# Attention outputs of a chunked linear-attention head as two 64-query halves in the array shape of k^T v

## The chip, the cores and the metric

The kernel runs on one core of a Trainium2 chip. Its time is that of one execution on the device in microseconds (us); three runs were made, and their median is the time before. The engines are TensorE (PE; its weight loads are listed as PEld), VectorE (DVE), ScalarE (ACT), GpSimd (POOL) and SyncE (SP, which issues the DMAs).

## The reference, cut to what matters

The program is a transformer block with adaptive layer norm on an input of 2 batches x 4096 tokens x 256 channels. Its attention part is two layers of a recurrent model (time mix and channel mix each), its second part a gated FFN with blockwise 4-bit rounding of inputs and weights. The change touches the recurrence of the time mix, for each of 4 heads of 64 channels:

```python
def step(state, inp):
    rt, kt, vt, wt = inp
    kv = kt[..., :, None] * vt[..., None, :]
    out = jnp.einsum('bhk,bhkv->bhv', rt, state + u[None, :, :, None] * kv)
    return (state * wt[..., None] + kv, out)
```

So each token's output is r times (the state of all earlier tokens plus the bonus u times its own k v^T), and the state decays by w per channel and takes k v^T in. Each head's output is then normalised over its 64 values.

## The kernel before, in words

Work is cut into tiles of 256 tokens (`TT`), 16 per batch and layer, and each tile into two chunks (`C`) of 128 tokens. With two layers and two batches there are 64 passes through the recurrence; one such pass of one tile, with all four heads, is called a head section here. The four heads stand in two pairs (`J`), a pair in the 128 partitions.

**Order of the work.** The kernel writes no instruction directly. Generators (one stream per batch and layer, and some for the FFN and the loading of weights) record operations through `Recorder` and `Plan.record` (L237); `Plan.run` (L342) chooses, again and again, the operation that can start first by its own table of costs (`weight`, L422, the latencies in `Plan.LAT`, and `TURN` and `BACK`, what a change of array shape costs) and issues it through `give_out` (L283, the call at L294, which is the line of almost all instructions in the profile). Calls to TensorE that one stream records without another engine's call or a `yield` between them become one operation and are issued in one burst. Each engine takes its instructions in the order issued. What the planner's table says of costs decides the order of all engines, not of the changed part alone.

**The head section** is `wkv` (L845). The streams take turns in it by `head_lock` while it is recorded. The decayed r and k are built level by level on VectorE; products of 32 or 64 keys with 16 to 64 queries land in the PSUM tile `pa`; masked copies put them, through `diag`, into `attn` (L675), a tile [128 keys, pair member p, chunk c, pair j, 128 queries] in SBUF. Four transposes (L936) bring k^T-to-be into a bank, and ScalarE copies it to `kt` (L939).

Then come (L950 to L975):
- `kv`: for each chunk, pair and head p, kt (128 tokens x 64) against v (128 x 64). The result of head p lies in partitions 64p to 64p+63, so the product uses 128 rows and 64 columns of the array, and the two heads of a pair use its two column halves.
- `po`, one PSUM bank of two chunks x 256: for each chunk and pair, r times the state S (a 128x128 product with 128 moving columns, which opens the accumulation), then per head attn (128 keys x 128 queries, the full array) times v (64 moving columns) on top.
- per chunk, after its outputs: the update of S on VectorE, S * decay + kv; chunk 1's r times S needs that of chunk 0. Then the square of the chunk's outputs on ScalarE and its sum per head on VectorE.

After both chunks: the power -1/2 on POOL, the scaling on VectorE, and back in `time_mix` transposes, the gate and the product with Wo.

All of it is fp32. A product in fp32 is seen in the trace as two records of weight load and two of matmul.

Of the kernel before, what the change touches and what calls it, by code (L numbers as in the profile page):

```python
# [11 lines left out]
BF16 = mybir.dt.bfloat16  # L12
I32 = mybir.dt.int32
AF = mybir.ActivationFunctionType
ALU = mybir.AluOpType
AX = mybir.AxisListType
PSUM = bass.MemoryType.PSUM

P = 128
D = 256  # L20
J = D // P
TT = 256
C = TT // P
HS = 64
H = D // HS
# [92 lines left out]
class Plan:  # L118
# [118 lines left out]
    def record(self, eng, fn, a, k):  # L237
        st = self.cur
        outs = [k["out"]] if "out" in k else [a[0]]
        ins = list(a[0 if "out" in k else 1:]) + [v for n, v in k.items() if n != "out"]  # L240
        ins = [v for v in ins if isinstance(v, (bass.AP, Later))]
        cost, port = weight(eng, fn, outs[0], ins)
        op = st.last if eng == "tensor" else None
        if op is None or op.next is None:
            self.count += 1
            op = Op(eng, self.count)
            op.rank = op.age + self.random.uniform(0.0, JITTER)
            op.late = st.late
            st.queue.append(op)
        st.last = op if eng == "tensor" else None  # L250
        op.calls.append((getattr(getattr(self.nc, eng), fn), a, k))
        f = form(eng, fn, outs[0], ins, a)
        if f is not None:
            if op.forms and op.forms[-1] != f:
                op.cost += self.TURN[eng]
            op.forms.append(f)
        op.cost += cost
        op.port = op.port or port
        for v in ins:
            if not is_dram(v):  # L260
                self.need(op, v, False)
        for v in outs:
            if not is_dram(v):
                self.need(op, v, True)
# [157 lines left out]
def weight(eng, fn, out, ins):  # L422


    def psum(v):
        return isinstance(v, Later) or v.name.startswith(("pa", "kv"))

    n = max(v.free_size() for v in [out] + ins)
    if eng == "tensor":
        n, rows, cols = out.free_size(), ins[0].shape[0], out.shape[0]  # L430
        if fn == "transpose":
            return 110.0, False
        if rows == P and cols == P:
            return max(4 * n / 2.4 + 6, 195.0 if n == 64 else 265.0 if n == P else 0.0), False
        if n <= 64:
            return {(64, 32): 18.0, (64, 64): 65.0, (P, 64): 65.0}.get((rows, cols), 2 * n), False
        return 0.57 * (4 * n / 2.4 + 6), False
    if eng == "sync":
        return 100.0, False
    wide = [v for v in ins if v.free_size() > 1]  # L440
    if eng == "scalar":
        return 180.0 + n / 1.2 + (85.0 if len(wide) < len(ins) else 0.0), False
    if eng == "gpsimd":
        if out.free_size() <= 8:
            return 360.0 + 170.0 * n, False
        return 90.0 + 2.1 * n, True
    two = sum(not psum(v) for v in wide) >= 2
    if fn in ("tensor_scalar", "tensor_copy"):
        two = not any(psum(v) for v in wide)
        if out.dtype == I32:  # L450
            return 145.0 + n / 1.92, two
    if fn in ("bn_stats", "bn_aggr", "tensor_reduce", "reciprocal"):
        two = False
    if fn == "reciprocal":
        return 150.0 + 6.2 * n, False
    return (205.0 if fn == "scalar_tensor_tensor" and n <= 256 else 150.0) + n / 0.96, two
# [3 lines left out]
def rwkv_adaln_fp4_kernel(ctx: ExitStack, tc: tile.TileContext, a: dict, out: bass.AP):  # L460
# [13 lines left out]
    nc = tc.nc  # L474
# [5 lines left out]
    const = ctx.enter_context(tc.tile_pool(name="const", bufs=1))  # L480
# [5 lines left out]
    make_identity(nc, ident)  # L486
    nhalf = const.tile([P, C * H], F32, name="nhalf")
    nc.gpsimd.memset(nhalf, -0.5)

# [37 lines left out]
    pl = Plan(nc, banks)  # L529
# [8 lines left out]
    def take_slot():  # L538
        return pl.take(stock)
# [4 lines left out]
    def give(*ts):  # L544
        stock.extend(ts)

    def give2(t):
        stock2.append(t)

    def v3(t, k=2):  # L550
        return t[:, : J * TT].rearrange("p (k n) -> p k n", k=k)

    def v4(t):
        return t[:, : J * TT].rearrange("p (c j t) -> p c j t", c=C, j=J)
# [59 lines left out]
    def halves(ps, k=2):  # L614
        return ps[:, :512].rearrange("p (k n) -> p k n", k=k)
# [38 lines left out]
    rows = {}  # L654
# [20 lines left out]
    attn = keep.tile([P, 2, C, J, P], F32, name="attn")  # L675
# [8 lines left out]
    def mm(o, lhsT, rhs, start, stop):  # L684
        pl.tensor.matmul(o, lhsT, rhs, start=start, stop=stop)
# [10 lines left out]
    head_lock = []  # L696
# [108 lines left out]
    def parts(rk):  # L805

        return (
            rk[:, m * J * TT : (m + 1) * J * TT].rearrange("p (c j t) -> p c j t", c=C, j=J) for m in range(2)
        )
# [35 lines left out]
    def wkv(i, b, rk_s, dec_s, v_s):  # L845

        S = state[i][b]
        rk = rk_s[:, : 2 * J * TT]
        dec, v = v4(dec_s), v3(v_s)
        yield from take(head_lock, (i, b))  # L850
        late = pl.cur.late
# [4 lines left out]
        r, k = parts(rk)  # L856
# [7 lines left out]
        tots_s = take_slot()  # L864
# [22 lines left out]
        for l in range(7):  # L887
            h = 1 << l
# [5 lines left out]
            n = C * J * P // (2 * h)  # L894
# [30 lines left out]
        r, k = parts(rk)  # L925
        tot = tot.rearrange("p (c j) -> p c j", c=C)
        for q in range(4):
            qs = slice(32 * q, 32 * (q + 1))
# [8 lines left out]
        kt_s = take_slot()  # L937
# [4 lines left out]
        o_s, sq_s = take_slot(), take_slot()  # L942
        o_sb, sq = v3(o_s), v3(sq_s)
        bk, po = pl.bank()
        po = halves(po)
        n = C * H
        few = pl.take(tiny)
        rs = few[:, :n]

        for c in range(C):  # L950
            for j in range(J):
                for p in range(2):
                    hd = slice((2 * j + p) * HS, (2 * j + p + 1) * HS)
                    mm(kv[p * HS : (p + 1) * HS, c, j, p * HS : (p + 1) * HS], kt[:, c, hd], v[:, c, hd], True, True)
        yield
        for c in range(C):
            for j in range(J):
                mm(po[:, c, j * P : (j + 1) * P], r[:, c, j, :], S[:, j, :], True, False)
                for p in range(2):
                    hd = slice((2 * j + p) * HS, (2 * j + p + 1) * HS)  # L960
                    mm(po[:, c, hd], attn[:, p, c, j, :], v[:, c, hd], False, p == 1)
            for j in range(J):
                pl.vector.scalar_tensor_tensor(
                    S[:, j, :], S[:, j, :], tot[:, c, j : j + 1], kv[:, c, j, :], ALU.mult, ALU.add
                )
            pl.scalar.activation(sq[:, c, :], po[:, c, :], AF.Square)
            pl.vector.tensor_reduce(
                rs[:, c * H : (c + 1) * H], sq[:, c, :].rearrange("p (h v) -> p h v", v=HS), AX.X, ALU.add
            )
            if c == C - 1:  # L970
                head_lock.clear()
                pl.cur.late = late
                give(kt_s, v_s, sq_s, tots_s)
                give2(rk_s)
            yield  # L975

        pl.vector.tensor_scalar(rs, rs, 1.0 / HS, EPS, ALU.mult, ALU.add)
        pl.gpsimd.tensor_tensor(rs, rs, nhalf[:, :n], ALU.pow)
# [9 lines left out]
    def time_mix(i, b, h):  # L988
# [116 lines left out]
        yield  # L1105

        o_s = yield from wkv(i, b, rk_s, dec_s, v_s)
        bk, pt = to_channels(v3(o_s))
        oT_s = o_s
# [363 lines left out]
```

## Time and profile before

| | |
|---|---|
| runs | 3097.47, 3093.93, 3090.12 us; median 3093.93 |
| span of the profiled execution (its own whole time is not marked among the runs) | 3081.1 us |
| mean granted TensorE clock | 0.981 |
| DMA over the span | 42.56 MB, mean 14 GB/s |
| update of S on VectorE | x256, 340 ns |
| sum of squares per chunk on VectorE (128x4 from 128x256) | x128, 414 ns |
| copy of a 128x512 bank to SBUF on ScalarE | x224, 588 ns |

How to read it: the span runs from the first to the last instruction. A busy share counts an engine as busy while any of its instructions is in flight; matmuls overlap, so their mean duration is a latency, and what a product costs TensorE in a dense row is the distance from its start to the next one's start. In a line of groups, "128*64 128x64 f32" means 128 rows and 64 columns of the array, then partitions and columns of the moving operand. The slices cut the span into 40 equal parts, a digit being tenths of busy time (or of the granted clock).

### The profile page before, as it was taken

The numbers are of one execution on the slowest core, as the hardware profiler recorded it, in microseconds if no ns is written. First come the engines' busy times: TensorE is split into PE (matmuls) and PEld (weight loads), VectorE is DVE, ScalarE is ACT, GpSimd is POOL, SyncE is SP. The second block draws the span as 40 slices with busy tenths as digits, with TensorE's granted clock in tenths as the row PEclk, the third lists the DMA queues.
The fourth block names the chain that finished last, engine by engine and source line by source line (L and its number), as shares of the span: only waits on it lengthen the run. The fifth ranks groups of instructions, "written<-read, shape, count | busy, mean of one in ns | idle before, by whom it ended". The sixth has DMA issues, their size and how long they took to land. (4 is left out here: it accounts for less than half of the span.)

```text
span 3081.1 us, 89987 instructions
## 1 busy us (share of the span) xinstructions
PE 2920.0 (95%) x38460; PEld 2388.7 (78%) x38460; DVE 2345.6 (76%) x6146; ACT 1667.6 (54%) x3478; POOL 1015.7 (33%) x1208
## 2 busy tenths in 40 slices
PE   6899999999999999999999999999999989999997
PEld 4678788777788887888778787787878778787775
DVE  6687876877787877878587777777778776777777
ACT  3465655564565656555564645646456454645452
POOL 2343333333333342333334233242323323232320
PEclk8899999999999999999999999999999999999999
DMA  4000000000000000000000000000000000000000
GB/s 141 12 19 9 15 7 16 3 16 7 13 12 4 20 3 13 11 8 15 5 18 4 10 13 4 19 5 19 4 8 15 3 20 3 6 11 9 9 14 11
DMA packets 35728, 42.56 MB, mean 14 GB/s; under 512 B 2816, under 2 KB 33536, under 8 KB 35328
## 3 DMA queue, kind: packets, MB, share of 16 engines
q1 hardware_dynamic: 35328, 36.81, 3.7%
q8 instruction: 302, 4.95, 0.6%
q14 instruction: 98, 0.80, 0.1%
HBM read 28.41 MB, written 8.39 MB: 12 GB/s over the span
## 5 line engine op out<-in xcount | busy, mean ns | idle before, releaser
L294 POOL TENSOR_TENSOR slot<-slot,slot 128x256 f32<-128x256 f32 (+1 forms) x768 | 578.1, 780 | 819.1 <-DVE slot L294 615.2
L294 ACT ACTIVATE slot<-bank 128x512 f32<-128x512 f32 (+2 forms) x644 | 334.3, 521 | 594.5 <-PE bank L294 563.4
L294 POOL TENSOR_TENSOR tiny<-tiny,nhalf 128x2 f32<-128x2 f32 (+1 forms) x288 | 296.9, 1034 | 874.6 <-DVE tiny L294 852.3
L294 PE MATMUL bank<-slot,cWk 128*128 128x256 f32 x1536 | 364.3, 385 | 4.5 <-DVE slot L294 4.5
L294 PE MATMUL bank<-slot,small 32*128 32x256 f32 (+3 forms) x2816 | 354.9, 359 | 10.3 <-DVE slot L294 6.9
L294 PE MATMUL bank<-cWv,slot 128*128 128x256 f32 x1536 | 342.4, 379 | 0.0
L294 PEld LDWEIGHTS bank<-slot,cWk 128*128 128x128 f32 x1536 | 288.1, 192 | 50.4 <-DVE slot L294 6.5
L294 ACT ACTIVATE slot<-bank,small 128x256 f32<-128x256 f32 (+1 forms) x640 | 250.9, 453 | 138.8 <-PE bank L294 128.7
L294 PEld LDWEIGHTS bank<-cWv,slot 128*128 128x128 f32 x1536 | 290.5, 190 | 39.7 <-issue 0.3
L294 PEld LDWEIGHTS bank<-slot,small 32*128 32x128 f32 (+3 forms) x2816 | 248.5, 178 | 86.2 <-issue 33.9
L294 DVE TENSOR_TENSOR slot<-slot,bank 128x512 f32<-128x512 f32 x192 | 130.7, 681 | 227.2 <-PE bank L294 193.5
L294 DVE TENSOR_TENSOR slot<-slot,slot 128x512 f32<-128x512 f32 x320 | 229.2, 718 | 82.2 <-PE pa L294 46.1
L294 DVE SCALAR_TENSOR_TENSOR slot<-bank,small,slot 128x256 f32<-128x256 f32 x640 | 265.1, 474 | 16.3 <-PE bank L294 16.0
L294 POOL TENSOR_TENSOR slot<-slot 128x512 f32<-128x512 f32 x128 | 140.3, 1098 | 358.4 <-ACT slot L294 253.5
L294 PEld LDWEIGHTS pa<-slot 64*32 64x32 f32 x11264 | 143.5, 109 | 79.9 <-DVE diag L294 35.2
L294 PE MATMUL pa<-slot 64*32 64x16 f32 x11264 | 171.6, 193 | 33.9 <-DVE diag L294 18.8
L294 PE MATMUL bank<-ident,slot 128*128 128x128 f32 x1152 | 176.1, 280 | 22.3 <-DVE slot L294 14.1
L294 DVE SCALAR_TENSOR_TENSOR slot<-slot,small,slot 128x256 f32<-128x256 f32 x384 | 183.4, 516 | 14.9 <-POOL slot L294 14.8
L294 ACT ACTIVATE slot<-slot 128x512 f32<-128x512 f32 x288 | 182.4, 636 | 21.9 <-DVE slot L294 17.3
L294 ACT ACTIVATE slot<-slot,tiny 128x256 f32<-128x256 f32 x256 | 141.6, 596 | 93.3 <-DVE tiny L294 89.9
L294 PE MATMUL bank<-wd,long 128*128 128x256 f32 x768 | 183.0, 389 | 2.2 <-ACT long L294 2.2
L294 PEld LDWEIGHTS bank<-ident,slot 128*128 128x128 f32 x1152 | 136.0, 143 | 57.8 <-DVE slot L294 19.6
(110 smaller groups left out, 5718.7 us busy)
## 6 DMA issues: line engine op xcount, KB each, us to landing
slot<-in_L_attn_x_dram SPq DMA_DIRECT2D x64, 256.0 KB, 2.8
out_dram<-slot SPq DMA_DIRECT2D x64, 128.0 KB, 1.7
slot<-in_L_wmod_dram SPq DMA_DIRECT2D x6, 256.0 KB, 7.7
cWk<-in_L_attn_cWk_dram SPq DMA_DIRECT2D x2, 768.0 KB, 8.1
cWv<-in_L_attn_cWv_dram SPq DMA_DIRECT2D x2, 768.0 KB, 9.4
small<-in_small_dram SPq DMA_DIRECT2D x2, 718.0 KB, 8.4
long<-in_L_ffn_w_down_dram SPq DMA_DIRECT2D x2, 352.0 KB, 2.8
long<-in_L_ffn_w_gate_dram SPq DMA_DIRECT2D x5, 128.0 KB, 2.2
```

The source lines that it names most:

```text
L294: fn(*[real(v) for v in a], **{n: real(v) for n, v in k.items()})
```

## The change

The attention outputs are no longer made with 128 queries in the full array, but as two products of 64 queries each (`q`), each in one column half of the array, the shape of the kv products. They are recorded right behind kv, without a `yield`, so that kv and they are one burst. Since r times S no longer comes first, two bf16 products of a constant tile of zeros (64 partitions x 512 columns each) open the accumulation in the whole bank. The four r times S products follow, two per chunk, chunk 1's after the update of S. The square and the sum per head are made once over both chunks, behind chunk 1. The planner's table gets a cost for bf16 products, 222 in place of 195 and 265 for the full-array products of 64 and 128 columns, and 59 in place of 65 for the 128x64 shape.

```diff
@@ weight
+        if ins[0].dtype == BF16:
+            return 0.5 * n / 2.4, False
         if rows == P and cols == P:
-            return max(4 * n / 2.4 + 6, 195.0 if n == 64 else 265.0 if n == P else 0.0), False
+            return max(4 * n / 2.4 + 6, 222.0), False
         if n <= 64:
-            return {(64, 32): 18.0, (64, 64): 65.0, (P, 64): 65.0}.get((rows, cols), 2 * n), False
+            return {(64, 32): 18.0, (64, 64): 65.0, (P, 64): 59.0}.get((rows, cols), 2 * n), False
@@ rwkv_adaln_fp4_kernel
     nc.gpsimd.memset(nhalf, -0.5)
+    zeros = const.tile([P, C * D], BF16, name="zeros")
+    nc.gpsimd.memset(zeros, 0.0)
@@ wkv
                     mm(kv[p * HS : (p + 1) * HS, c, j, p * HS : (p + 1) * HS], kt[:, c, hd], v[:, c, hd], True, True)
-        yield
+        for q in range(2):
+            mm(po[q * HS : (q + 1) * HS].rearrange("p c d -> p (c d)"), zeros[:, :HS], zeros, True, False)
         for c in range(C):
             for j in range(J):
-                mm(po[:, c, j * P : (j + 1) * P], r[:, c, j, :], S[:, j, :], True, False)
                 for p in range(2):
                     hd = slice((2 * j + p) * HS, (2 * j + p + 1) * HS)
-                    mm(po[:, c, hd], attn[:, p, c, j, :], v[:, c, hd], False, p == 1)
+                    for q in range(2):
+                        qs = slice(q * HS, (q + 1) * HS)
+                        mm(po[qs, c, hd], attn[:, p, c, j, qs], v[:, c, hd], False, False)
+        yield
+        for c in range(C):
+            for j in range(J):
+                mm(po[:, c, j * P : (j + 1) * P], r[:, c, j, :], S[:, j, :], False, c == C - 1 and j == J - 1)
             for j in range(J):
                 pl.vector.scalar_tensor_tensor(
                     S[:, j, :], S[:, j, :], tot[:, c, j : j + 1], kv[:, c, j, :], ALU.mult, ALU.add
                 )
-            pl.scalar.activation(sq[:, c, :], po[:, c, :], AF.Square)
-            pl.vector.tensor_reduce(
-                rs[:, c * H : (c + 1) * H], sq[:, c, :].rearrange("p (h v) -> p h v", v=HS), AX.X, ALU.add
-            )
-            if c == C - 1:
-                head_lock.clear()
-                pl.cur.late = late
-                give(kt_s, v_s, sq_s, tots_s)
-                give2(rk_s)
-            yield
+            yield
+        pl.scalar.activation(sq, po, AF.Square)
+        pl.vector.tensor_reduce(rs, sq_s[:, : C * D].rearrange("p (h v) -> p h v", v=HS), AX.X, ALU.add)
+        head_lock.clear()
+        pl.cur.late = late
+        give(kt_s, v_s, sq_s, tots_s)
+        give2(rk_s)
+        yield
```

More of the change, by code (lines that the diff above doesn't have):

```diff
@@ L954, in wkv @@
                     mm(kv[p * HS : (p + 1) * HS, c, j, p * HS : (p + 1) * HS], kt[:, c, hd], v[:, c, hd], True, True)
+        for q in range(2):
+            mm(po[q * HS : (q + 1) * HS].rearrange("p c d -> p (c d)"), zeros[:, :HS], zeros, True, False)
+        for c in range(C):
+            for j in range(J):
+                for p in range(2):
+                    hd = slice((2 * j + p) * HS, (2 * j + p + 1) * HS)
+                    for q in range(2):
+                        qs = slice(q * HS, (q + 1) * HS)
+                        mm(po[qs, c, hd], attn[:, p, c, j, qs], v[:, c, hd], False, False)
         yield
@@ L957, in wkv @@
             for j in range(J):
-                mm(po[:, c, j * P : (j + 1) * P], r[:, c, j, :], S[:, j, :], True, False)
-                for p in range(2):
-                    hd = slice((2 * j + p) * HS, (2 * j + p + 1) * HS)
-                    mm(po[:, c, hd], attn[:, p, c, j, :], v[:, c, hd], False, p == 1)
+                mm(po[:, c, j * P : (j + 1) * P], r[:, c, j, :], S[:, j, :], False, c == C - 1 and j == J - 1)
             for j in range(J):
```

## The prediction

> **What bounds the kernel now.** I read the page's first two parts, then the waits, the groups of TensorE by shape, and the timeline of one head.
>
> ```profile
> PE 2920.0 (95%) x38460; PEld 2388.7 (78%) x38460; DVE 2345.6 (76%) x6146; ACT 1667.6 (54%) x3478; POOL 1015.7 (33%) x1208
> ```
> ```profile
> PE   6899999999999999999999999999999989999997
> ...
> DVE  6687876877787877878587777777778776777777
> ...
> PEclk8899999999999999999999999999999999999999
> ```
> The matmul unit is busy in 90% or more of nearly every slice; VectorE has a quarter of its time free in most. The 161 us without a matmul (3081.1 - 2920.0) lie largely in the first two slices and the last two. So in the middle the time is the sum of what PE issues, plus short stalls. The waits agree: for PE the longest sums are
>
> ```profile
> PE bank L294 <- DVE slot L294: 43.2, 33, 13.8
> PE pa L294 <- DVE diag L294: 24.1, 28, 2.3
> ...
> PE kv L294 <- ACT slot L294: 7.1, 13, 1.4
> ```
> (total us, times, longest). None is large against 3081.
>
> The groups by shape (busy, mean ns of one):
>
> ```profile
> L294 PE MATMUL bank<-slot,attn 128*128 128x64 f32 x1024 | 146.6, 267 | 0.0
> ...
> L294 PE MATMUL bank<-S,slot 128*128 128x128 f32 x512 | 111.8, 301 | 4.4 <-ACT slot L294 2.2 <-DVE S L294 1.0 <-DVE slot L294 0.9
> ...
> L294 PE MATMUL kv<-slot,slot 128*64 128x64 f32 x1024 | 45.2, 232 | 7.9 <-ACT slot L294 7.1 <-issue 0.4
> ```
> Two things to see. Each fp32 product is two records: 512 calls of attn*v stand as x1024. And attn*v and k^T v move the same 64 columns in the same number of records, yet one group is busy 146.6 us and the other 45.2. The mean of one (267, 232) hides it: it is latency. What counts is the distance between starts, in the timeline of PE over a head that never waited:
>
> ```profile
> 2838.30 0.60 PE L294 MATMUL bank<-ident,slot 128*128 128x128 f32 x4
> 2838.73 0.39 PE L294 MATMUL bank<-S,slot 128*128 128x128 f32 x2
> 2838.96 0.56 PE L294 MATMUL bank<-slot,attn 128*128 128x64 f32 x4
> 2839.35 0.44 PE L294 MATMUL bank<-S,slot 128*128 128x128 f32 x2
> 2839.63 0.56 PE L294 MATMUL bank<-slot,attn 128*128 128x64 f32 x4
> 2840.11 0.69 PE L294 MATMUL kv<-slot,slot 128*64 128x64 f32 x16
> 2840.73 0.66 PE L294 MATMUL bank<-ident,slot 128*128 128x128 f32 x4
> 2841.46 0.46 PE L294 MATMUL bank<-S,slot 128*128 128x128 f32 x2
> 2841.75 0.56 PE L294 MATMUL bank<-slot,attn 128*128 128x64 f32 x4
> 2842.15 0.44 PE L294 MATMUL bank<-S,slot 128*128 128x128 f32 x2
> 2842.42 0.56 PE L294 MATMUL bank<-slot,attn 128*128 128x64 f32 x4
> ```
> Four attn records take 0.39 us (2838.96 to 2839.35), 0.10 each; sixteen kv records, alternately in the left and right 64 columns of the array, take (0.69 - 0.222)/15 = 0.031 each (0.222 is the median of one).
>
> **The change, per head** (64 heads: 2 layers, 2 batches, 16 tiles).
>
> Prices of turning the array: attn followed by kv costs 0.48 where attn followed by S costs 0.39, so +0.09 on leaving the full shape. kv's sixteen starts take 0.62 to the next group, against 16 x 0.031 = 0.50: some 0.10 on leaving kv. The first full-shape product after it pays 0.10 more: at 1415 us the eight cWr records right behind kv take 1.83 us, where eight records 0.216 apart (the usual distance of 256-column records) make 1.73. Both versions turn in and out once per head at least.
>
> Before: S 0.23 + 0.28 + 0.29 + 0.27 = 1.07; attn 4 x 0.40 = 1.60; turn in 0.09; kv 0.50; turn out 0.10 + 0.10. Sum 3.46 us.
>
> After:
> - Halves: 16 products are 32 records in kv's shape, 32 x 0.031 = 0.99.
> - kv: 0.50, unchanged. Turns 0.09 + 0.20, unchanged.
> - S: four products side by side. Between attn records, S takes 0.28; right behind transposes 0.23 (two steps of 0.112). Next to each other I take the latter: 4 x 0.224 = 0.90.
> - Zeros: two bf16 products of 512 columns, one record each. The trace has no bf16 matmul. Upper end: the fp32 rate, 256 columns in 0.216, makes 0.43 a record; if the two halves of the array did not overlap, 0.86, and a turn of 0.09 on either side if the change of type counts as one: 1.04. Lower end: both hidden but for two starts of 7 ns (the smallest distance of kv's records): 0.01. A gain is excluded, nothing is taken away. I take 0.22: half the fp32 rate, since a bf16 column has half the bytes, with the halves overlapped as kv's are. This is an estimate from those rows.
>
> [...]
>
> Sum after 0.99 + 0.50 + 0.29 + 0.90 + 0.22 = 2.90. Saved 0.56 a head, 36 us in all.
>
> [...] The trace first: kv's records start 0.031 apart on average, half of them only 7 ns apart. [...]
>
> **What else moves.**
> - The order. Costs in the planner's table change, so it deals out all work anew. Counted over the two programs' PE orders, shape changes go from 968 to 988 and returns to the full array from 409 to 433: 20 x 0.095 + 24 x 0.10 = +4 us.
> - The wait on the copy of k^T. Before, S and attn of chunk 0 stand between the four transposes and kv (1.81 us in the timeline, 2838.30 to 2840.11), and hide ScalarE's copy (row mean 0.588). Now the whole burst is queued behind that copy, and PE takes its instructions in order: everything behind it waits. The need is about 0.95 from the last transpose's start (0.27 of its latency, 0.59 of copy, 0.1 of signals). In the new order other streams' products fill the gap: counted with the distances above, in 59 heads 0.64 us or more stand there, most often 1.39, and in 5 heads only 0.20. The copy of attn's diagonal comes earlier and is waited for likewise. Price: 5 heads with 0.2 of cover lose 0.75, the others little: +4 us, +5 with them. Against it stand the 7.1 us above, which are lost on this copy now, from ScalarE being late; a longer cover saves some of it. Net +2.
> - State update. S of chunk 1 waits for VectorE's update. Fill between is under 1.1 us in 15 heads, before in 9: +3.
> - Square and reduce over both chunks at once: ScalarE 2 x 0.385 becomes 0.596, VectorE 2 x 0.414 becomes 0.674 (rows of these sizes), 11 and 10 us less on engines with room: nothing gained. But the last chunk's chain is 0.21 + 0.26 = 0.47 us later, covered by the other streams; uncovered in every head, 30 us.
> - attn, v and k^T come free earlier: a small gain, at 0.
> - One memset of 128x512 bf16 at the start of POOL's queue, ahead of the iotas that VectorE's masks wait for, which precede the first loads: 0.31 by the row of a 128x256 f32 memset of the same bytes (0.16 to 0.96 by the smaller and larger memsets). +0.3. No DMA is added; SP's queue is only reordered.
>
> Sum: -36 + 4 + 2 + 3 + 0.3 = -27 us. The profiled span is 3081.1; the median of the runs is 3093.93, so 12.8 lie around the span (the profiled execution's own whole time is not marked). 3081.1 - 27 + 12.8 = **3067 us**.
>
> **Rivals.** (0.2%, 6 us, is about what a measurement here can tell from no change.)
> 1. Zeros at the fp32 rate, 0.43: 13 us of the gain go, 3080. Speaks for: no bf16 row. Against: half the bytes. Still faster.
> 2. Another engine keeps the pace: VectorE, with 76%, or the head's longer tail (0.47 x 64 = 30 us). PE's 27 us turn into idle time, 3092: the same. Against: slices of PE at 9 throughout, PE's waits on VectorE few.
> 3. Slower: missing cover at the burst. The filler ahead of the burst is taken from other places, and ScalarE's copy comes late. Each head without cover loses 0.95; the gain is gone at 27/0.95, some 28 of 64 heads, and at 40 heads the time is 3067 + 38 = 3105. For: kv waits already under 1.81 us of own cover. Against: 59 heads have filler in the order.
> 4. Stalls shrink as well, kv's and others': 3050.
>
> **How the numbers follow.** Forecast 0.60, rival 1 0.10, rival 2 0.12, rival 3 0.12, rival 4 0.06. Faster 0.60 + 0.10 + 0.06 = 0.76, same 0.12, slower 0.12. Beside the gain, the stalls of a new order may differ by some 15 us, about a tenth of the 161 us without a matmul. The range runs from 3043, rival 4 and half of that, to 3097, rivals 1 and 2 with some of it; it leaves out rival 3 and thin tails, under 2 in 10. The upper end of the zeros, 1.04, would give 3067 + 52 = 3119; it is thought unlikely and left out with rival 3.
>
> **What would show it.** The attn group becomes x2048 in shape 128*64 at some 0.03 between starts (wrong: 0.06 or more); the zeros' two records take 0.2 up to the first half (wrong: 0.4 or more); S records stand 0.112 apart; PE's busy time falls by some 25 to 35 us; PE's wait for ScalarE before kv stays under 15 us (rival 3: 30 or more); PE's slices stay at 9 (rival 2: 8 and less).

## The result and the profile after

The changed kernel takes 3129.45 us (median of 4 runs) against 3092.56 (4 runs) before: ratio 1.0121, 95% interval 1.0103 to 1.0138. It is slower by 1.2%, where 0.9% faster was forecast, and lies above the range. The profiled execution took 3131.42 us with a span of 3129.2, so only 2.2 us lie around a span; the 12.8 of the prediction came from setting a short profiled execution (3081.1) beside longer timed ones. Executions of one kernel differ by up to 15 us, and the granted clock with them: later ones of the kernel before run from a span of 3084.0 us at a clock of 0.981 to 3099.0 at 0.976, so about 10 us of a difference between two profiles below can be this.

What was done to TensorE came out much as worked out. This is the timeline of PE over one head that did not wait, in the changed kernel (start us, busy us, shape, count):

```profile
2451.96 0.69 PE L294 MATMUL kv<-slot,slot 128*64 128x64 f32 x16
2452.47 0.39 PE L294 MATMUL bank<-zeros 128*64 128x512 bf16 x2
2452.69 1.10 PE L294 MATMUL bank<-slot,attn 128*64 128x64 f32 x32
2453.72 0.71 PE L294 MATMUL bank<-S,slot 128*128 128x128 f32 x4
2454.36 0.70 PE L294 MATMUL pa<-slot 64*32 64x16 f32 x62
...
2455.55 0.71 PE L294 MATMUL bank<-S,slot 128*128 128x128 f32 x4
2456.10 1.89 PE L294 MATMUL bank<-slot,cWk 128*128 128x256 f32 x8
```
From start to start: kv 0.51, zeros 0.22, halves with the turn out 1.03, S 0.64 with its turns and 0.55. Sum 2.95 us a head; the turn into kv's shape, 0.09 by the prediction, lies ahead of the first row and has to be added: 3.04 where 2.90 was predicted. And still the span grew by 48 us (37 by the medians). The first part of the page says where:

```profile
PE 2915.4 (93%) x39612; PEld 2353.6 (75%) x39612; DVE 2340.9 (75%) x6082; ACT 1648.9 (53%) x3406; POOL 1011.8 (32%) x1209
```
PE is busy 2915.4 us, 4.6 less than before, and idle 3129.2 - 2915.4 = 213.8, where it was 161.1: 52.7 more. That makes the 48. Its 40 slices hardly show it; the middle ones stay at 9:

```profile
PE   6899999999999999999999999999999999899887
```
Two waits of PE before (total us, times, longest):

```profile
PE bank L294 <- POOL slot L294: 14.9, 14, 3.2
PE bank L294 <- DVE long L294: 11.6, 7, 6.8
```
and the waits of PE in the changed kernel:

```profile
PE bank L294 <- DVE slot L294: 42.7, 21, 14.8
PE bank L294 <- DVE long L294: 31.1, 11, 6.8
PE pa L294 <- DVE diag L294: 25.3, 25, 2.2
PE bank L294 <- POOL slot L294: 25.0, 22, 2.5
...
PE kv L294 <- ACT slot L294: 10.9, 15, 1.5
```
The wait that was feared, kv on the copy of k^T, grew from 7.1 to 10.9 only. The largest growth is in a place that the change does not touch: the FFN's transposes waiting for VectorE (`long`, 11.6 to 31.1). Products waiting for POOL come next (14.9 to 25.0); most of that growth is ahead of the product with Wo (9.8 to 18.3), which follows the head section and its longer tail. One wait on `long`, in the timeline of all engines:

```profile
1721.82 2.32 PE L294 MATMUL bank<-Wo,slot 128*128 128x256 f32 x10
...
1725.30 0.87 DVE L294 SCALAR_TENSOR_TENSOR long<-long,long 128x704 f32<-128x704 f32 x1
...
1727.75 0.67 DVE L294 TENSOR_TENSOR slot<-slot,bank 128x512 f32<-128x512 f32 x1
...
1729.42 0.86 DVE L294 SCALAR_TENSOR_TENSOR long<-long,scales 128x704 f32<-128x704 f32 x1
...
1730.33 1.54 PE L294 MATMUL bank<-ident,long 128*128 128x128 f32 x6 [6.19 <-DVE long L294]
```
For 6.19 us PE has nothing to do but the next product in its queue, and VectorE is busy all that time, with other streams' work between two steps of the one result that PE waits for. The wait costs twice, in idle time and in clock. Busy time and granted clock of ten-microsecond stretches around it (PE busy, PEld, DVE, ACT, POOL, then the clock):

```profile
1710.00:1720.00 10.00, 8.54 (x45) 6.89 (x43) 5.77 (x14) 3.19 (x8) 1.73 (x2) 1.00 0.00 0
1720.00:1730.00 10.00, 3.72 (x16) 2.91 (x16) 9.93 (x24) 1.46 (x3) 4.37 (x5) 0.85 0.10 26
1730.00:1740.00 10.00, 9.67 (x50) 8.06 (x51) 4.73 (x15) 4.88 (x11) 2.80 (x3) 0.80 0.00 1
```
The clock drops within the wait (1.00, 0.85, then 0.80 when PE is busy again), and the next products run slowly: the last five starts of the six records behind it lie 0.21 us apart, where records of this group at full clock start 0.109 apart (median). Over the span the mean clock is 0.972 after 0.981 before:

```profile
core 0: 3129.2 us, clock 0.972
```
so 0.028 x 3129 = 88 us of full clock are lost where 0.019 x 3081 = 59 were: 29 us more. Not all of it costs time, since PE is idle in a part of it. By the trace's clock records PE is busy for 137.8 us at half clock in the changed kernel, for 103.0 before; half of the difference, 17 us, makes busy time longer, an estimate from the starts in a dense row (records of 256 columns of `bank<-slot,cWk` start 0.427 us apart at half clock, 0.216 at full, medians). Reckoned at full clock (half of the busy time at half clock taken off) PE is busy 2846.5 us after 2868.5: its work did fall, by 22 us, and 17 of these went to the clock. So 22 less work, 17 of clock and 52.7 of idle time make the 48.

### The profile page after: what moved, and what is told of

The parts are those of the page before. It is cut to its first block, busy times and chain, and to the rows that moved or that the text cites. A ratio compares the mean times of both kernels' runs of the same rounds, so it can differ in the third digit from the quotient of the medians.

```text
span 3129.2 us, 92097 instructions
## 1 busy us (share of the span) xinstructions
PE 2915.4 (93%) x39612; PEld 2353.6 (75%) x39612; DVE 2340.9 (75%) x6082; ACT 1648.9 (53%) x3406; POOL 1011.8 (32%) x1209
## 4 chain that ended last, share of the span: by engine, by line
PE 67%; DVE 18%; ACT 10%; issue 2%; POOL 1%; DMA 1%; SPq 0%; POOLq 0%; ACTq 0%; DVEq 0%
PE bank L294 61%; DVE slot L294 8%; PE pa L294 5%; ACT slot L294 4%; DVE long L294 4%; ACT rk L294 2%; ACT attn L294 2%; DVE tiny L294 2%; DVE rk L294 1%; ACT L294 1%; DVE diag L294 1%; DVE scales L294 1%; PE kv L294 1%; POOL slot L294 1%; ACT long L294 1%
## 5 line engine op out<-in xcount | busy, mean ns | idle before, releaser
L294 ACT ACTIVATE slot<-bank 128x512 f32<-128x512 f32 (+2 forms) x580 | 321.4, 559 | 609.5 <-PE bank L294 582.4
L294 POOL TENSOR_TENSOR tiny<-tiny,nhalf 128x2 f32<-128x2 f32 (+1 forms) x288 | 290.1, 1010 | 842.1 <-DVE tiny L294 819.4
L294 PE MATMUL bank<-ident,slot 128*128 128x128 f32 x1152 | 176.0, 284 | 25.5 <-DVE slot L294 16.5
L294 DVE TENSOR_TENSOR long<-long,bank 128x352 f32<-128x352 f32 x256 | 131.3, 515 | 85.7 <-ACT long L294 67.6
```

The lines of the kernel that those rows point to most:

```text
L294: fn(*[real(v) for v in a], **{n: real(v) for n, v in k.items()})
```

## The experiments

Three theories. **O**: the half-products are as cheap as the distances say, and the loss lies in the order that the planner dealt anew. **W**: the burst behind the copy of k^T makes the loss, in any order. **R**: half-products cost more than the distances show.

### The products exchanged, the order kept

For these runs the planner records the kernel's own operations, and only the calls inside a recorded operation are replaced, behind the planner's reckoning of its cost. So every engine's order stays that of the kernel named. The table of costs is changed only together with the products, in the dealt orders; no run has the one without the other.

`b_halves`, in the order of the kernel before, inside each chunk's operation:

```diff
+            part = pl.cur.last.calls
...
+            part[:] = [part[0], (part[3][0], part[3][1], dict(start=False, stop=False))]
+            for h in range(H):
+                hd = slice(h * HS, (h + 1) * HS)
+                for q in range(2):
+                    qs = slice(q * HS, (q + 1) * HS)
+                    part.append((nc.tensor.matmul, (po[qs, c, hd], attn[:, h % 2, c, h // 2, qs], v[:, c, hd]), dict(start=False, stop=h == H - 1)))
```

> The order of all instructions is that of the kernel before, on every engine; only the products within chunk c's own operation are exchanged: both r times S, then eight half-products in the 128x64 shape on top (no zeros, since r times S opens each chunk). Theory O (the products are as cheap as their start distances say, and the loss lies in the order that the planner dealt anew): attn 1.60 becomes 0.99 us and S 1.07 becomes 0.90 a head, one more turn in and out 0.29, so 0.49 x 64 = 31 us less than before, some 3062. Theory W (the burst's wait behind the copy of k^T makes the loss in any order): the same 3062, since S and attn still stand ahead of kv here. Theory R (half-products cost PE more than the distances show, by weight loads or by bank conflicts): 3092 or more.

Measured 3086.2 us against 3091.05: ratio 0.9982 (0.9971 to 0.9994). It is 5 us, not 31.

`b_burst`, the same order; chunk 0's operation takes a full-shape product of zeros, S of chunk 0 and all 16 halves, chunk 1's is S alone:

```diff
+            part = pl.cur.last.calls
...
+            part[:] = [(part[3 * j][0], part[3 * j][1], dict(start=False, stop=c == C - 1 and j == J - 1)) for j in range(J)]
+            if c == 0:
+                part.insert(0, (nc.tensor.matmul, (po.rearrange("p c d -> p (c d)"), zeros[:, :P], zeros), dict(start=True, stop=False)))
+            for d in range(C if c == 0 else 0):
...
+                        part.append((nc.tensor.matmul, (po[qs, d, hd], attn[:, h % 2, d, h // 2, qs], v[:, d, hd]), dict(start=False, stop=False)))
...
```

> The order of the kernel before again. Chunk 0's operation becomes: one bf16 product of zeros over the bank in the full shape, r times S of chunk 0, all 16 half-products of both chunks; kv follows in the same shape in nearly all heads; chunk 1's operation is r times S alone. Square and sum are made once over both chunks, behind chunk 1. Theories O and W: S 0.90, zeros 0.22, halves 0.99, kv and turns as before, 0.56 x 64 = 36 us less than before, some 3056. Theory R: 3092 or more. If the later Square and sum (0.47 us a head) were what costs: up to 30 us of it back, 3086.

Measured 3088.31 against 3091.05: 0.9993 (0.998 to 1.0007), no difference. PE is busy 19 us less than before (2900.9) and idle 31 us more (this profiled execution is 6 us above the median). All theories but R had expected 31 to 36 us. But R is refuted: reckoned at full clock PE is busy 23 us less than before in `b_halves` and 33 less here, so the products are nearly as cheap as worked out (31 and 36), and what they save does not reach the end. `a_full` below says the same. Nor is it the later Square and sum, for which 3086 had been named: `b_halves` keeps both per chunk and comes to the same time.

`b_late`, the same order with the change's own sequence, everything behind kv:

```diff
...
+                        behind.append((nc.tensor.matmul, (po[qs, d, hd], attn[:, h % 2, d, h // 2, qs], v[:, d, hd]), dict(start=False, stop=False)))
...
+                kv_calls.append((second, (behind,), {}))
```
(`second` issues the zeros, the halves and S of chunk 0 with whichever of kv and chunk 0's operation comes second, which is kv in nearly all heads; the other call of it issues nothing.)

> As the run before it, in the order of the kernel before, but with the change's own sequence: kv first, then two bf16 zeros in the 128x64 shape, the 16 half-products and r times S of chunk 0, all behind the copy of k^T. The planner does not know of it, so no other stream's work is put ahead of the burst. All theories expect the wait on the copy to show here: about 0.95 less 0.2 a head, 62 heads, 45 us above the run with the halves ahead of kv, some 3100; PE's wait on ScalarE before kv rises from 7 to 40 us or more. If it stays under 3070, the wait is no part of the loss at all (against theory W).

Measured 3171.84: 1.026 (1.0227 to 1.0293), 83 us above `b_burst`. The waits of PE and of VectorE in this run:

```profile
PE kv L294 <- ACT slot L294: 65.3, 59, 2.7
```
```profile
DVE S L294 <- PE bank L705: 120.0, 58, 6.2
```
So the sequence is dear where the planner does not know of it: PE waits for the copy 59 times, 63 us more than in `b_burst` (2.3), and VectorE's queue stands still ahead of the update of S (132 us in all, 63 in `b_burst`). Theory W is right that there is such a price; on the copy the changed kernel doesn't pay it, as its 10.9 us show.

`a_full`, in the order of the changed kernel, with 128 queries in the full array again:

```diff
+        burst = pl.cur.last.calls
...
+        burst[8:] = [(nc.tensor.matmul, (po.rearrange("p c d -> p (c d)"), zeros[:, :P], zeros), dict(start=True, stop=False))]
+        for c in range(C):
+            for h in range(H):
+                hd = slice(h * HS, (h + 1) * HS)
+                burst.append((nc.tensor.matmul, (po[:, c, hd], attn[:, h % 2, c, h // 2, :], v[:, c, hd]), dict(start=False, stop=False)))
```

> The order of the changed kernel on all engines; only the burst's products are exchanged: kv, then one bf16 product of zeros in the full shape and the eight attn products with 128 queries in the full array; S as in the change. Theory O and W: the halves' gain goes, 1.60 - 0.99 = 0.61 x 64 = 39 us; the changed kernel's 3129 becomes 3150 to 3168 (less where PE's longer products fill stalls). Theory R: 3129 or less.

Measured 3182.3: 1.0294 (1.0263 to 1.0325) of the kernel before, 53 us more than the changed kernel. Here the halves are worth 53 us (36 of it PE's busy time at full clock, 39 had been expected), in the order before 3 to 5. Theory R falls. Theory O is right that the products are cheap and that the loss of 37 goes with the order, but the 31 to 36 us that it expected in the order before came to 3 to 5.

### Is TensorE the bound at all?

`b_none` and `b_twice` keep the order before and leave the attn products out, or make them twice (shown: left out; the other doubles those calls in the same list):

```diff
+            part = pl.cur.last.calls
...
+            part[:] = [(part[3 * j][0], part[3 * j][1], dict(start=True, stop=True)) for j in range(J)]
```

> The order of the kernel before on all engines, with the attn times v products left out (the output lacks each chunk's inner part; r times S opens and closes the bank alone). It removes 1.60 us of TensorE's work a head, 103 us in all, and 0.78 us of chunk 0's cover ahead of kv, which gives back up to 0.3 x 64 = 20 us. If TensorE's work is the bound: about 3010. If the order is bound by chains through several engines as well (which would explain the 31 us that came to 5): 3050 or more.

> The order of the kernel before, with each attn times v product made twice (the inner part of the output counts double): 103 us more of TensorE's work. If TensorE is the bound, or any delay of it is paid in full: 3091 + 100 = 3190. If there is slack beside it: 3120 to 3160.

Measured 3075.24 and 3188.44 (one run each), against 3095.72 in the same session. Taking 103 us of products away brings 20; adding 103 costs 93. Part of the asymmetry was counted in: without its own cover kv waits again,

```profile
PE kv L294 <- ACT slot L294: 35.5, 51, 2.3
```
where 7.1 were lost before, which is 28 us of the 83 that are missing. The rest is new idle time elsewhere and clock. The first lines of the two runs:

```profile
span 3073.4 us, 87928 instructions
...
PE 2846.0 (93%) x37436; PEld 2292.2 (75%) x37436; DVE 2343.3 (76%) x6146; ACT 1661.7 (54%) x3478; POOL 1016.3 (33%) x1208
```
```profile
span 3186.6 us, 92035 instructions
...
PE 3035.4 (95%) x39484; PEld 2510.5 (79%) x39484; DVE 2353.7 (74%) x6146; ACT 1671.8 (52%) x3478; POOL 1016.1 (32%) x1208
```

The ledger of these runs, each from its profile: idle is span less PE busy, lost clock is span x (1 - mean granted clock), and the last column is PE's busy time reckoned at full clock, an estimate from the trace's clock records as above (it falls by 101 us where 103 are left out, and grows by 112 where 103 are added).

| run | span | PE busy | PE idle | lost clock | PE busy at full clock |
|---|---|---|---|---|---|
| before | 3081.1 | 2920.0 | 161.1 | 59 | 2868.5 |
| halves, order before (`b_halves`) | 3087.4 | 2902.9 | 184.5 | 65 | 2845.5 |
| burst, order before (`b_burst`) | 3092.6 | 2900.9 | 191.7 | 77 | 2835.5 |
| no attn products (`b_none`) | 3073.4 | 2846.0 | 227.4 | 89 | 2767.7 |
| attn products twice (`b_twice`) | 3186.6 | 3035.4 | 151.2 | 64 | 2981.0 |
| changed kernel | 3129.2 | 2915.4 | 213.8 | 88 | 2846.5 |
| changed, full array (`a_full`) | 3182.6 | 2969.9 | 212.7 | 105 | 2882.6 |

In the order before, what PE no longer does turns into idle time and lost clock: in `b_none` 101 us of work are gone by the last column, PE is idle 66 us more, and 27 us are lost because more of the rest is done at half clock (157 us busy there, 103 before). At the places where PE arrives early, the input is not ready. That chains through VectorE, ScalarE and POOL end there at nearly the same time is our reading: kv's wait on ScalarE apart, the growth is spread over many small waits, and no run takes work from those engines.

### The same kernels in other orders

The planner adds a small random part to each operation's rank (`JITTER`), drawn from a seed, and both kernels use seed 0. Another seed gives the same work in another order (of the counts by engine only ScalarE's varies, by its table loads: 107 in the changed kernel, 117 with seed 1):

```diff
-    best = min(range(PLANS), key=lambda seed: plan(seed, True))
+    best = min(range(1, 1 + 1), key=lambda seed: plan(seed, True))
```

> The changed kernel, with another seed of the planner's small random part (up to 8 in an operation's rank): the same instructions, dealt in another order. Theory O (the sequence of the head is good, seed 0 only got a bad order): the orders scatter by 20 us or so and the changed kernel's mean lies below that of the kernel before; this one could lie at 3050 to 3110. Theory W (the burst behind the copy, and VectorE's update of S behind the burst, cost time in any order): 3115 to 3140.

> The kernel before with seed 1. Theory O: seed 0 was a good draw, this one lies above 3091 by 10 to 40 us. Theory W: within 10 us of 3091.

> The changed kernel with seed 2. As for seed 1: theory O 3050 to 3110, theory W 3115 to 3140.

> The kernel before with seed 2. As for seed 1: theory O 3100 to 3130, theory W 3081 to 3101.

> The changed kernel with seed 3, to see the scatter over orders. So far seeds 0, 1, 2 gave 3129, 3083 and 3105 (mean 3106). Theory O: 3075 to 3135, the mean of four below that of the kernel before by 10 to 30 us.

> The kernel before with seed 3. So far seeds 0, 1, 2 gave 3090, 3127 and 3160 (mean 3126). Theory O: 3095 to 3160, above seed 0 again. If it lies under 3090, seed 0 is no good draw and theory O is weak.

> The changed kernel with seed 4. The kernel before gave 3090, 3127, 3160, 3110, 3127 with seeds 0 to 4 (mean 3123), the changed one 3129, 3083, 3105, 3115 so far. Theory O: 3080 to 3120, which leaves the changed kernel's mean of five 10 to 30 us under the other; above 3150 the two would not differ on average.

> The kernel before with seed 4. Theory O: above seed 0 once more, 3100 to 3160 (seeds 0 to 3 gave 3090, 3127, 3160, 3110).

| seed | before | changed |
|---|---|---|
| 0 | 3092.6 (median of 4) | 3129.5 (median of 4) |
| 1 | 3126.7 | 3083.1 |
| 2 | 3160.4 | 3104.7 |
| 3 | 3109.9 | 3114.7 |
| 4 | 3127.2 | 3079.2 |
| mean | 3123 | 3102 |

(One run each but for seed 0.) Orders of one kernel lie up to 68 us apart. Seed 0 is the best of five for the kernel before and the worst of five for the changed one. That the result has the sign it has comes from this pair: in three of the other four pairs the changed kernel is the faster. On the mean of five it is 21 us faster, near the 27 predicted, but with standard deviations of 25 and 21 that mean has an error of about 15: it is not shown that the change gains on average, only that the loss of 37 is no property of its instructions. Why seed 0 is so good for the kernel before, by chance or because its other constants were chosen with this seed, no run shows.

### The half-products first

If kv is to be covered by the head's own work, the half-products can go ahead of it, since they need attn only, and S behind it:

```diff
+        for q in range(2):
+            mm(po[q * HS : (q + 1) * HS].rearrange("p c d -> p (c d)"), zeros[:, :HS], zeros, True, False)
+        for c in range(C):
+            for h in range(H):
...
+                    mm(po[qs, c, hd], attn[:, h % 2, c, h // 2, qs], v[:, c, hd], False, False)
+        yield
         for c in range(C):
             for j in range(J):
...
                     mm(kv[p * HS : (p + 1) * HS, c, j, p * HS : (p + 1) * HS], kt[:, c, hd], v[:, c, hd], True, True)
-        for q in range(2):
...
         yield
...
```

> The change in another sequence, dealt out by the planner, seed 1: zeros and half-products first, in one operation of their own that needs attn only; then kv, which needs the copy of k^T and is now covered by 1.2 us of the head's own work in the same shape; then r times S. If part of the change's loss is the burst behind the copy (theory W beside O), PE's wait for ScalarE before kv falls from 10.9 us to under 5, and the mean over seeds lies 10 to 30 us under that of the changed kernel (3106); by theory O alone it scatters about 3106 as before.

> The same with seed 2. Theory W beside O: 3075 to 3100 on average of the two; theory O alone: about 3106 with 20 us of scatter.

> Half-products first, then kv, then r times S, with the seed that the planner's own table reckons shortest of 18. Theory O, with orders as the larger lever: 3060 to 3085, faster than the kernel before and than the changed one. If the planner's table says nothing of the chip, it scatters about 3100.

> The changed kernel as it is, with the seed that the planner's table reckons shortest of 22. If the seed is the lever: 3060 to 3080, like the version with the half-products first (3063). If the sequence with the half-products first is: above 3090.

Measured: 3087.42, 3091.12 and, with the chosen seed, 3063.38, which is 0.9895 (0.9878 to 0.9911) of the kernel before: 1.1% faster, the best version here. Its profile:

```profile
span 3062.2 us, 92134 instructions
...
PE 2890.3 (94%) x39612; PEld 2343.4 (77%) x39612; DVE 2341.1 (76%) x6082; ACT 1672.6 (55%) x3428; POOL 1013.8 (33%) x1209
```
PE is busy 30 us less than before and idle 171.9, 11 more; the lost clock is 58, about as before (59). Here the work saved does reach the end. Seeds 1 and 2 lie where W beside O had them (3075 to 3100), but the changed kernel's own seeds 1 and 2 average 3094, 5 us from them. The expected fall of kv's wait to under 5 is a miss: 8.8, 7.0 and 10.5 us with the three seeds, 10.9 in the change. The changed kernel with its own chosen seed (`a_seed12`) came to 3087.38, 0.9977 (0.9963 to 0.9991): just faster than before, not 3060 to 3080. A seed alone did not make 3063, then; whether the sequence or luck made the last 24 us stays open, with three orders of the one and six of the other.

## Why the prediction was wrong, point by point

- **Prices on PE: nearly right.** Halves, kv, zeros, S and turns were to make 2.90 us a head and make 3.04 with the turn in. The term that is too low is S: the four products were priced as standing next to each other (0.90), but chunk 1's stand apart, behind other streams' products in another shape, and with their turns the two pairs take 0.64 + 0.55. That leaves 0.42 saved a head, 27 us, and less the 4 that were counted for extra turns 23: near the 22 found at full clock, where 36 - 4 = 32 were predicted. The zeros' two records take 0.22 in all, the value taken, though no run shows that the bytes are the reason; the upper ends (0.43, 1.04) are out, and with them rival 1. Half-products start 1.03 / 32 = 0.032 apart with the turn counted in, well under the 0.06 that was named as a sign of being wrong.
- **Wait on the copy: right** (+2 predicted; 7.1 to 10.9). The cover by other streams' products held. Rival 3 ended on the right side by the wrong mechanism; `b_late` shows its price, 83 us, more than the 45 expected: 63 are the wait before kv itself, and how much of the rest comes from VectorE's longer wait isn't shown.
- **Wait for the update of S: too high.** PE waited 0.8 us for it in all, not 3 more. VectorE's wait for PE ahead of the update was overlooked (25.5 us before, 62.5 after); the fastest version has as much of it, so it decides nothing by itself.
- **"In the middle the time is the sum of what PE issues, plus short stalls": this step failed.** A busy share of 95% and slices of 9 were read as a bound. The reading behind it was wrong too: the 161 us without a matmul do not lie largely in the first and last two slices, which hold 66 of them; 95 lie in the 36 slices between, over three times the gain that was forecast. And "slices stay at 9", named as a sign of being right, came true in a slower kernel. `b_none` shows otherwise: of 103 us taken away 20 arrive. `b_twice` shows why one takes it for a bound: delays arrive nearly in full. In this order a saving on PE was worth little and a delay much.
- **"The stalls of a new order may differ by some 15 us": mis-sized**, and this term alone carries the sign. The re-dealt order was priced by its extra turns (+4) and given 15 us of scatter; five orders of one kernel span 68 us before and 50 after. That the order at hand could be a good draw was not thought of. In the changed kernel the new order's stalls came to 52.7 us of idle time and 17 of clock lost in busy time (some 10 of the sum because the profile before is a short one).
- Rival 2 (another engine keeps the pace, no change) has the number that the fixed-order runs gave: 3086 and 3088 for 3091. It had 0.12. No single engine is shown to keep the pace, and its second half, the head's longer tail, shows only in the 8.5 us more that Wo's products wait for POOL.

## What to carry to other kernels

A busy share of 95% said here that delays will be paid, not that savings will be; leave the work out in the same order, and look what arrives, before pricing a saving. Where a planner or scheduler deals out the order, a change in any cost deals it anew: measure the scatter over several orders of the same kernel first, and judge a change by means over orders or in an order held fixed. And when the instructions are better but the total is worse, draw more orders before the change is dropped.

## What the runs showed of the hardware

The granted clock was lower beside long waits, and the products behind them ran slower: around the 6.19 us wait above it was 1.00, 0.85 and 0.80 in stretches of ten microseconds. Over the span PE was busy at half clock for 137.8 us, after 103.0 before, which by the estimate above made its busy time 17 us longer. The trace of the changed kernel has the granted clock at one half in 28 stretches, 9 of them 3.4 us long, 16 of 6.8, one of 10.2 and two of 13.7, and each of the four longest waits of mid-run (3.8 to 6.7 us) has one of 6.8 us beside it. But not every stretch has so long a wait: 7 of the 28 have a wait of over 3 us beside them; beside the other 21 the longest wait is 0.4 to 2.7 us. In the 3.4 us ahead of a drop PE was busy for a share of 0 to 0.78. So the clock fell beside short waits as well; what makes it fall is not shown. The prediction has no term for the clock: over these runs the lost clock goes from 58 us (the fastest) to 105 (`a_full`).

Two bf16 products of 512 columns in the two column halves of the array start 6 to 7 ns apart in 60 of 64 heads of the changed kernel and take 0.22 us together (0.215 to 0.216 to the first half-product in 59 heads), and no turn is seen between fp32 and bf16 records of the same shape: from kv's first record to the zeros it is 0.515 us in 55 heads, where sixteen records 0.031 apart make 0.50.
